# Graph stack on one core: the end of layers 0 and 1 in another order, piece loads issued by ScalarE, stores and indices by SyncE, first loads of the recurrence in parts

## The chip, the cores and the metric

The kernel runs on one core of one Trainium2 chip. A core has TensorE (PE in the profile), VectorE (DVE), ScalarE (ACT), GpSimd (POOL) and SyncE (SP), and 16 DMA engines to which SP, ACT and POOL can give transfers. The metric is the device time of one execution in microseconds (us); lower is better.

## The reference

Sixteen graphs (B = 16) of 1024 nodes (N) with 256 features (D) pass through four layers, in float32. Each layer adds its output to x. All weights and the dense adjacency matrix `adj` (about 3% of its entries are not zero) are inputs.

```
for each layer: h = relu(layernorm(x)); x = x + layer(h)
layer 0: u = adj * exp(e_i + f_j + a_b); a = u / row sum of u; out = a @ (h W_w^T + W_b)
layer 1: d = (row sum of adj + 1e-5)^-0.5; out = d_i adj d_j @ (h weight) + bias
layer 2: for i in 0 .. N-1, one after the other:
             p = (adj^T scaled by 1/deg)[i] @ h        # uses the rows of h already replaced
             r, z = sigmoid(split(x_i W_ioux^T + b + p W_iouh^T + b'))
             hc = tanh(x_i W_coux^T + b + (p * r) W_couh^T + b')
             h[i] = z * p + (1 - z) * hc
layer 3: out = silu(rmsnorm(((eps h + adj @ h) W1 + b1))) W2 + b2
```

## The kernel before, in words

`layers_0_1` computes layers 0 and 1 and prepares layer 2; in the profiled execution it fills about 1463 of 4587 us. `layer_2` is the recurrence, then layer 3 follows. The text calls an iteration of `layers_0_1` a stage.

**Stages.** The loop over i has a stage for each graph. `sums` multiplies the adjacency of graph i with a 1024 x 256 operand in seven products of quarters (a Strassen-like scheme: the quarters `b11`, `b21`, `b22`, `t1` to `t4` are tiles `at`, products go to the PSUM banks `px`, `py`, `pz`, sums to `ag`). It is called twice a stage: with the operand of layer 0 (tile `q`) and with that of layer 1 (tile `h1`). The operand's differences s1 and s2 are made by VectorE in `combos` (L358, L359); product "s2" is the third, and begins with a matmul named px<-at,s. In `sums` (L374 is the matmul) ScalarE copies px into `ag` (L380, L387, L393) and VectorE adds or subtracts the other banks (L384, L394, L398, L401).

**Hooks.** `sums` takes seven functions, one called after each product: a0, a1, a2_, a3 to a6 in the first call, d0 to d6 in the second. They hold everything else a stage does: loads of the next graph (`load_x`, `get`), statistics (`Moments`), additions of quarters by an accumulating DMA of POOL (`plus`, L294), and `plus_row` (L349), which adds a row vector to a quarter of x on POOL: `W_b` for layer 0, `bias` for layer 1, four pairs each.

**After each call.** `weights` (L410, L413) multiplies `ag` by the layer's weights and adds to x: layer 0 of graph i after the first call, layer 1 of graph i - 1 there too (`second_weights`), in pairs of node tiles. `normed` (L345, ScalarE) gives h1, and, after the second call, h2 of graph i - 1, the input of layer 2. `inv_sqrt` (L83, POOL) makes the scales `rs`. x after layer 1 is stored to `x2_d` (L707), h2 to `he_d` (L789).

**An order for the recurrence.** The generator `orders` runs beside the stages on VectorE: `side(us)` in a hook takes its next steps up to a cost. `places` puts the 128 nodes of each node tile into bins (o_fit L129 to L134); `rest` (L155 and on) makes indices, stores them to `order_d` (L176), reads them back as `table` (L181), then makes a second assignment (L197, L198) and picks (o_top, o_open, o_most, o_need). Both read a part of the adjacency, `own`, in pieces of four rows of `pc` (256 KB): `fetch` (L101) issues one, two ahead of its use in `piece` (L106); three buffers hold them. Of 64 pieces, 32 are for `places`, 32 for `rest`.

**Jobs.** From stage 9 on a `Job` for each graph prepares layer 2's data, two a stage (run_a and run_b): `load` (L490, L492, L495), `mask` and `scale` (on POOL, L503 to L511), `turn` (permutes h2 by transposes, L521 to L526, and stores `heT_d`, L527), `first` (L533), `order` (L545 to L556: permutes adjacency tiles, stores `near_d` and `next_d`), `base` (L562 to L565, stores `base_d`). Jobs 14 and 15 come in a last iteration i = 16, after the second sums of graph 15: the tail. All of these stores are issued by POOL.

**The recurrence's start.** `layer_2` issues on SP the loads of its weights (`wx`, L821), biases, `he` (L950, from heT_d), `bxt` (L1156, from base_d) and `wh`; `hs<-he` (L991) on POOL feeds its first matmuls (L1000).

Each engine runs its instructions in the order in which the program writes them (`manual_schedule`); waits between engines and for tile buffers follow from the data.

Of the kernel before, what the change touches and what calls it, by code (L numbers as in the profile page):

```python
# [16 lines left out]
P = 128  # L17
# [23 lines left out]
def gnn_stack(ctx: ExitStack, tc: tile.TileContext, a: dict, out: bass.AP):  # L41
# [51 lines left out]
    def orders(pool, psum):  # L93
# [5 lines left out]
        def fetch(j0):  # L99
            nz = pool.tile([P, R, P], F32, name="pc", bufs=3)  # L100
            nc.gpsimd.dma_start(nz, a["own"][:, j0 : j0 + R])  # L101
            pieces.append(nz)
# [14 lines left out]
        def places():  # L117
# [4 lines left out]
            fetch(0)  # L122
            fetch(R)
            yield 9.0
            for j0 in range(0, P, R):
# [12 lines left out]
                if j0 + 2 * R < P:  # L138
                    fetch(j0 + 2 * R)
# [15 lines left out]
        def rest():  # L155
# [14 lines left out]
            for k in range(2):  # L170
# [8 lines left out]
                with nc.allow_non_contiguous_dma(reason="indices, once"):  # L179
                    for g in range(G2):  # L180
                        nc.gpsimd.dma_start(table[k][:, g].rearrange("p t s -> p (t s)"),  # L181
                                            order_d[k].rearrange("t s b i -> (b i) (t s)")[g * GR : (g + 1) * GR])
# [7 lines left out]
            fetch(0)  # L190
            fetch(R)
            yield 9.0
            for j0 in range(0, P, R):
# [8 lines left out]
                if j0 + 2 * R < P:  # L202
                    fetch(j0 + 2 * R)
# [48 lines left out]
        yield from places()  # L252
        yield from rest()
# [5 lines left out]
    def layers_0_1():  # L259
        with ExitStack() as st:  # L260
# [13 lines left out]

            load_x(0, 2)
            we = big.tile([P, DC, D + 1], F32, name="ad")
# [200 lines left out]
            class Job:  # L477
# [51 lines left out]
                def first(self):  # L529
# [6 lines left out]
                    del h2[b]  # L536
# [30 lines left out]
                def rest(self):  # L567
                    self.first()
                    self.order()
                    self.base()  # L570

            math = orders(big, psum)
            left = [0.0]

            def side(us):
                left[0] += us * 1.25
                while left[0] > 0:
                    cost = next(math, None)
                    if cost is None:
                        break  # L580
                    left[0] -= cost
                left[0] = min(left[0], 0.0)
# [36 lines left out]
            jobs[16] = (Job(14, {"ao": "at5"}), Job(15, {"ad": "at0", "ab": "at1", "to": "at2", "hT": "at3", "ao": "at4"}))  # L619

            for i in range(B + 1):
# [4 lines left out]
                def a0():  # L626
# [4 lines left out]
                    if i:  # L631
                        plus_row(x[i], "W_b", 1)
                    side(1.0)
                def a1():
                    if ahead:
                        get(i + 1, "b11", 0, 0)
                    if i:
                        plus_row(x[i], "W_b", 2)
                    second()
                    add_halves(i, "t4", "t2", "b21")  # L640
                def a2_():
                    if ahead:
                        get(i + 1, "t1", 0, 1)
                    if i:
                        plus_row(x[i], "W_b", 3)
                    side(3.4)
                def a3():
                    side(2.6)
                def a4():
                    if ahead:  # L650
# [27 lines left out]
                else:  # L678
                    run_a.load()
                    run_b.load()  # L680
                    run_a.mask()
                    run_a.scale()
                last = i == B
                mv2 = small.tile([P, NT, 2], F32, name="mv")

                def second_weights(pairs):
                    if behind:
                        weights(x[i - 1], ags[i - 1], w1, dis[i - 1],
                                (lambda t: stats(x[i - 1], (t,), mv2)) if last else (lambda t: None), pairs)
                pairs = list(range(0, NT, 2))  # L690
                if run_a:
                    run_a.turn()
                else:
                    second_weights(pairs[:2])
                    pairs = pairs[2:]
                if here:
# [6 lines left out]
                    if ahead:  # L703
                        mean[i + 1].root()
                second_weights(pairs)
                if behind:
                    nc.gpsimd.dma_start(rows(x2_d[i - 1]), x[i - 1])  # L707
                if last:
                    rs2 = inv_sqrt(small, mv2[:, :, 1], LN_EPS, [P, NT], "rs")
                    run_a.rest()  # L710
                    shift = small.tile([P, NT], F32, name="shift")
# [953 lines left out]
```

## Time and profile before

| what | value |
|---|---|
| median of three runs | 4593.31 us (4590.48, 4593.31, 4597.71) |
| profiled execution, its own time | 4588.57 us |
| its span in the trace | 4586.7 us |
| granted TensorE clock, mean | 0.974 |
| stages 1 to 8 start at | 99.6, 178.0, 256.1, 334.8, 412.8, 491.6, 562.9, 641.0 us |
| stages 9 to 15 start at | 712.3, 802.4, 908.5, 1017.2, 1126.2, 1226.0, 1325.2 us |
| second sums of graph 15 end | 1398.5 us |
| first load of the recurrence (wx, L821) issued | 1463.65 us |

The page's first section gives each engine's busy time, its share of the span, and the number of instructions. In the lists of waits each line names the engine and line that waited, what ended the wait, the total in us, the number of times and the longest. In a timeline a line is: start in us, duration in us, engine, source line, operation, output<-input, count. A line such as L374 is one of the kernel's file. The profile comes from one execution, so sums made from it stand against that execution's own time.

### The profile page before, as it was taken

The numbers are of one execution on the slowest core, as the hardware profiler recorded it, in microseconds if no ns is written. First come the engines' busy times: TensorE is split into PE (matmuls) and PEld (weight loads), VectorE is DVE, ScalarE is ACT, GpSimd is POOL, SyncE is SP. The second block draws the span as 40 slices with busy tenths as digits, with TensorE's granted clock in tenths as the row PEclk, the third lists the DMA queues.
The fourth block names the chain that finished last, engine by engine and source line by source line (L and its number), as shares of the span: only waits on it lengthen the run. The fifth ranks groups of instructions, "written<-read, shape, count | busy, mean of one in ns | idle before, by whom it ended". The sixth has DMA issues, their size and how long they took to land. (4 is left out here: it accounts for less than half of the span.)

```text
span 4586.7 us, 55389 instructions
## 1 busy us (share of the span) xinstructions
PE 4255.1 (93%) x18967; PEld 2921.0 (64%) x18967; DVE 2718.0 (59%) x6213; ACT 1606.4 (35%) x3861; POOL 1653.1 (36%) x1880
## 2 busy tenths in 40 slices
PE   7999999888896999999999999999799999999998
PEld 3544455444554777777777878787556656565656
DVE  7888877577752444444444444446366666666765
ACT  2454545333432232322232323233233343333333
POOL 2232323543434323232323323324243444444352
PEclk9999999999997999999999999999899999999999
DMA  5354446766546544444344444541232222222310
GB/s 190 119 155 152 148 137 204 211 221 220 202 159 212 163 141 151 145 148 153 126 142 152 127 156 146 166 135 63 74 130 91 103 83 101 92 92 85 109 47 19
DMA packets 355108, 627.15 MB, mean 137 GB/s; under 512 B 42016, under 2 KB 259744, under 8 KB 336288
## 3 DMA queue, kind: packets, MB, share of 16 engines
q1 hardware_dynamic: 314208, 462.36, 30.2%
q0 software_dynamic: 40480, 159.68, 11.4%
q8 instruction: 204, 3.34, 0.3%
q14 instruction: 216, 1.77, 0.1%
HBM read 488.52 MB, written 116.65 MB: 132 GB/s over the span
## 5 line engine op out<-in xcount | busy, mean ns | idle before, releaser
L888 PE MATMUL pf<-hb,ab 128*128 128x256 f32 x1568 | 407.9, 383 | 16.5 <-DMA hb<-hs_d 7.2
L1000 PE MATMUL pf<-hs,wx 128*128 128x256 f32 x1536 | 349.8, 382 | 22.4 <-POOL hs L991 20.8
L1000 PEld LDWEIGHTS pf<-hs,wx 128*128 128x128 f32 x1536 | 291.3, 192 | 65.9 <-POOL hs L991 22.6
L888 PEld LDWEIGHTS pf<-hb,ab 128*128 128x128 f32 x1568 | 280.5, 191 | 68.6 <-issue 14.0
L1454 PE MATMUL ph<-bxt,hb 128*128 128x512 f32 x704 | 312.4, 600 | 6.4 <-ACT hb L1438 5.6
L1483 POOL TENSOR_TENSOR ss<-ss,sq 128x512 f32<-128x512 f32 x224 | 280.5, 1271 | 88.6 <-ACT sq L1481 84.9
L83 POOL TENSOR_TENSOR rs<-rs_v,mhalf 128x8 f32<-128x8 f32 (+1 forms) x65 | 112.4, 1729 | 551.8 <-DVE rs_v L79 368.8
L410 PE MATMUL pmm<-w,ag 128*128 128x256 f32 x1024 | 242.2, 393 | 33.7 <-DVE x L413 17.4
L1288 POOL DMA_INDIRECT hs_d<-h,table x128 | 128.9, 1007 | 339.6 <-ACTq L1274 162.5
L410 PEld LDWEIGHTS pmm<-w,ag 128*128 128x128 f32 x1024 | 196.9, 196 | 80.8 <-DVE x L413 29.8
L1544 PEld LDWEIGHTS po<-w,hh 128*128 128x128 f32 x2048 | 236.0, 193 | 9.5 <-issue 7.2
L1544 PE MATMUL po<-w,hh 128*128 128x128 f32 x2048 | 240.2, 277 | 1.4 <-ACT hh L1527 0.7
L1454 PEld LDWEIGHTS ph<-bxt,hb 128*128 128x128 f32 x704 | 133.8, 193 | 168.2 <-issue 160.8
L1005 DVE TENSOR_TENSOR gates<-pf,bias 128x512 f32<-128x512 f32 x128 | 88.2, 690 | 237.8 <-PE pf L1000 237.8
L1526 DVE TENSOR_TENSOR hh<-hh,po 128x512 f32<-128x512 f32 x256 | 154.4, 678 | 96.7 <-PE po L1523 96.7
L1095 ACT ACTIVATE r<-pr 128x256 f32<-128x256 f32 (+3 forms) x230 | 68.0, 347 | 403.1 <-PE pr L1054 387.7
L1481 ACT ACTIVATE sq<-hh 128x512 f32<-128x512 f32 x224 | 141.2, 630 | 164.3 <-DVE hh L1479 125.3
L1036 PE MATMUL pf<-bd,h 128*128 128x384 f32 (+4 forms) x512 | 185.8, 455 | 4.6 <-ACT bs L875 2.8
L1039 DVE TENSOR_TENSOR bxt<-bxt,pf 128x384 f32<-128x384 f32 (+4 forms) x256 | 124.8, 500 | 97.6 <-PE pf L1036 96.1
L1479 DVE SCALAR_TENSOR_TENSOR hh<-ph,b,u 128x512 f32<-128x512 f32 x192 | 144.0, 751 | 64.8 <-PE ph L1475 54.5
L1112 DVE TENSOR_TENSOR w<-w,hc 128x256 f32<-128x256 f32 (+3 forms) x230 | 87.4, 380 | 138.8 <-ACT hc L1111 138.7
L337 ACT ACTIVATE pt<-x,m_neg 128x256 f32<-128x256 f32 x240 | 114.3, 476 | 151.1 <-DVE m_neg L332 144.8
(351 smaller groups left out, 9528.5 us busy)
## 6 DMA issues: line engine op xcount, KB each, us to landing
at<-in_quarters SPq DMA_DIRECT2D x80, 1024.0 KB, 11.5
ab<-in_columns SPq DMA_DIRECT2D x127, 512.0 KB, 3.8
bxt<-in_adjT SPq DMA_DIRECT2D x88, 512.0 KB, 5.9
at<-at POOLq DMA_DIRECT2D x30, 1024.0 KB, 8.9
at<-in_adjT SPq DMA_DIRECT2D x40, 512.0 KB, 6.8
pc<-in_own POOLq DMA_DIRECT2D x64, 256.0 KB, 6.7
x_d<-x POOLq DMA_DIRECT2D x16, 1024.0 KB, 4.9
he_d<-h POOLq DMA_DIRECT2D x16, 1024.0 KB, 12.8
```

Of the source, the lines that this page charges most:

```text
L410: nc.tensor.matmul(po[:, t - t0], ag[:, c, t * P : (t + 1) * P], w[:, c], start=c == 0, stop=c == DC - 1)
L888: nc.tensor.matmul(pb, ab[:, jts[k]], hb[:, jts[k]], start=k == 0, stop=k == len(jts) - 1)
L1000: nc.tensor.matmul(pg[:, e], wx[:, c, q * D + e * P : q * D + (e + 1) * P], self.hs[:, c], start=c == 0, stop=c == DC - 1)
L1036: nc.tensor.matmul(pf, h[:, g, c * P : (c + 1) * P], bd[:, g, b0 : b0 + n, S : S + far], start=True, stop=True)
L1039: return lambda: nc.vector.tensor_add(to, to, pf)
L1288: nc.gpsimd.indirect_dma_start(out=hs_d[t][g][:, :], out_offset=row(1, g, t, s), in_=h[:, g], in_offset=None)
L1454: nc.tensor.matmul(pa, h[b][:, mt, c * P : (c + 1) * P], at[b][n0 // NH][:, mt], start=mt == 0, stop=mt == NT - 1)
L1479: nc.vector.scalar_tensor_tensor(hh[q][:, k], ph, b1[:, k : k + 1], u, op0=ALU.add, op1=ALU.add)
L1481: nc.scalar.activation(sq, hh[q][:, k], AF.Square)
L1483: nc.gpsimd.tensor_tensor(ss[q], ss[q], sq, ALU.add)
L1526: nc.vector.tensor_mul(hh[q][:, k], hh[q][:, k], pr)
L1544: nc.tensor.matmul(po[:, n], left[:, c, n * P : (n + 1) * P], right[:, c], start=onto is None and n == 0 and c == 0, stop=c == HH - 1, ski ...
```

## The change

1. `fetch` hands its load to a list, `later`, which the next `side` empties; ScalarE issues it (`nc.scalar.dma_start`). Three pieces are fetched ahead in place of two; the buffers stay three.
2. The stores to `x2_d` and `he_d` and the loads of `table` are issued by SP in place of POOL. Each of the four loads of `table` is followed by a step boundary of cost 5.0.
3. `plus_row` moves: W_b pairs 1 to 3 from a0, a1, a2_ to a2_, a3, a4; bias pairs 0 to 3 from d0 to d3 to d2, d3, d4, d6.
4. In stages 9 to 15 `run_a.turn` stands after `normed` of h1, between the two halves of `second_weights`, in place of ahead of them.
5. Iteration i = 16 is gone. After the second sums of graph 15 an order written out by hand runs jobs 13, 14 and 15 in turns, with buffers named for them.
6. In `layer_2` the loads of `he` for t = 0 and of `bxt` are split by graph: 0 to 13, 14, 15.
7. The setup tile `we` takes a buffer of the name "x".

The core of the diff:

```diff
@@ -97,9 +97,11 @@
         def fetch(j0):
-            nz = pool.tile([P, R, P], F32, name="pc", bufs=3)
-            nc.gpsimd.dma_start(nz, a["own"][:, j0 : j0 + R])
-            pieces.append(nz)
+            def run():
+                nz = pool.tile([P, R, P], F32, name="pc", bufs=3)
+                nc.scalar.dma_start(nz, a["own"][:, j0 : j0 + R])
+                pieces.append(nz)
+            later.append(run)
@@ -119,8 +121,8 @@
             nc.vector.memset(held, 0.0)
-            fetch(0)
-            fetch(R)
+            for j0 in range(0, 3 * R, R):
+                fetch(j0)
             yield 9.0
@@ -135,8 +137,8 @@
                         yield 1.0
-                if j0 + 2 * R < P:
-                    fetch(j0 + 2 * R)
+                if j0 + 3 * R < P:
+                    fetch(j0 + 3 * R)
                 yield 1.2
@@ -176,10 +178,11 @@
                 yield 9.0
-                with nc.allow_non_contiguous_dma(reason="indices, once"):
-                    for g in range(G2):
-                        nc.gpsimd.dma_start(table[k][:, g].rearrange("p t s -> p (t s)"),
-                                            order_d[k].rearrange("t s b i -> (b i) (t s)")[g * GR : (g + 1) * GR])
+                for g in range(G2):
+                    with nc.allow_non_contiguous_dma(reason="indices, once"):
+                        nc.sync.dma_start(table[k][:, g].rearrange("p t s -> p (t s)"),
+                                          order_d[k].rearrange("t s b i -> (b i) (t s)")[g * GR : (g + 1) * GR])
+                    yield 5.0
@@ -249,8 +252,12 @@
-        yield from places()
-        yield from rest()
+        later = deque()
+
+        def work():
+            yield from places()
+            yield from rest()
+        return work(), later
@@ -272,8 +279,8 @@
+            we = big.tile([P, DC, D + 1], F32, name="x", bufs=3)
             load_x(0, 2)
-            we = big.tile([P, DC, D + 1], F32, name="ad")
             nc.sync.dma_start(we[:, :, :D], a["W_w"].rearrange("(c p) d -> p c d", p=P))
@@ -533,7 +540,6 @@
                     nc.scalar.activation(self.bs, pb[:, :D], AF.Copy, scale=dinv[:, b, 0:1])
-                    del h2[b]
@@ -568,11 +574,14 @@
                     self.base()
-
-            math = orders(big, psum)
+                    del h2[self.b]
+
+            math, later = orders(big, psum)
             left = [0.0]
...
             def side(us):
+                while later:
+                    later.popleft()()
                 left[0] += us * 1.25
@@ -616,9 +625,11 @@
             jobs = {i: (Job(2 * (i - 9)), Job(2 * (i - 9) + 1)) for i in range(9, 16)}
-            jobs[16] = (Job(14, {"ao": "at5"}), Job(15, {"ad": "at0", "ab": "at1", "to": "at2", "hT": "at3", "ao": "at4"}))
-
-            for i in range(B + 1):
+            jobs[15][1].names = {"ao": "h1"}
+            job14 = Job(14, {"ad": "at6", "ab": "ds", "to": "at0", "hT": "q", "ao": "hT"})
+            job15 = Job(15, {"hT": "h1", "ao": "q"})
+
+            for i in range(B):
                 run_a, run_b = jobs.get(i, (None, None))
@@ -628,25 +639,25 @@
                         run_a.load()
-                    if i:
-                        plus_row(x[i], "W_b", 1)
                     side(1.0)
...
                         get(i + 1, "b11", 0, 0)
-                    if i:
-                        plus_row(x[i], "W_b", 2)
                     second()
...
                     if i:
-                        plus_row(x[i], "W_b", 3)
+                        plus_row(x[i], "W_b", 1)
                     side(3.4)
                 def a3():
+                    if i:
+                        plus_row(x[i], "W_b", 2)
                     side(2.6)
                 def a4():
+                    if i:
+                        plus_row(x[i], "W_b", 3)
                     if ahead:
@@ -675,24 +686,13 @@
                     rs = inv_sqrt(small, mv[:, :, 1], LN_EPS, [P, NT], "rs")
-                else:
-                    run_a.load()
-                    run_b.load()
-                    run_a.mask()
-                    run_a.scale()
-                last = i == B
-                mv2 = small.tile([P, NT, 2], F32, name="mv")
...
                     if behind:
-                        weights(x[i - 1], ags[i - 1], w1, dis[i - 1],
-                                (lambda t: stats(x[i - 1], (t,), mv2)) if last else (lambda t: None), pairs)
+                        weights(x[i - 1], ags[i - 1], w1, dis[i - 1], pairs=pairs)
                 pairs = list(range(0, NT, 2))
-                if run_a:
-                    run_a.turn()
-                else:
-                    second_weights(pairs[:2])
-                    pairs = pairs[2:]
+                second_weights(pairs[:2])
+                pairs = pairs[2:]
                 if here:
@@ -702,22 +702,11 @@
                         mean[i + 1].root()
+                if run_a:
+                    run_a.turn()
                 second_weights(pairs)
                 if behind:
-                    nc.gpsimd.dma_start(rows(x2_d[i - 1]), x[i - 1])
-                if last:
-                    rs2 = inv_sqrt(small, mv2[:, :, 1], LN_EPS, [P, NT], "rs")
-                    run_a.rest()
-                    shift = small.tile([P, NT], F32, name="shift")
-                    nc.vector.scalar_tensor_tensor(shift, mv2[:, :, 0], -1.0, rs2, op0=ALU.mult, op1=ALU.mult)
-                    h2[i - 1] = big.tile([P, NT, D], F32, name="h2", bufs=2)
-                    normed(h2[i - 1], x[i - 1], shift, rs2, all_)
-                    nc.gpsimd.dma_start(rows(he_d[i - 1]), h2[i - 1])
-                    run_b.mask()
-                    run_b.scale()
-                    run_b.turn()
-                    run_b.rest()
-                    break
+                    nc.sync.dma_start(rows(x2_d[i - 1]), x[i - 1])
                 if run_a:
@@ -732,19 +721,17 @@
                         get(i + 1, "t3", 0, 1)
-                    plus_row(x[i], "bias", 0)
                     if m2:
...
                 def d1():
-                    plus_row(x[i], "bias", 1)
                     second1()
...
                 def d2():
-                    plus_row(x[i], "bias", 2)
+                    plus_row(x[i], "bias", 0)
                     if m2:
@@ -752,12 +739,13 @@
                 def d3():
-                    plus_row(x[i], "bias", 3)
+                    plus_row(x[i], "bias", 1)
                     if ahead:
...
                 def d4():
+                    plus_row(x[i], "bias", 2)
                     if ahead:
@@ -772,10 +760,13 @@
                 def d6():
+                    plus_row(x[i], "bias", 3)
                     if m2:
...
                 ags[i] = sums(i, left_of, [d0, d1, d2, d3, d4, d5, d6], lambda name: drop(i, name))
+                if not ahead:
+                    break
                 if run_b:
@@ -786,7 +777,7 @@
                     normed(h2[i - 1], x[i - 1], m2.shift, m2.rs, all_)
-                    nc.gpsimd.dma_start(rows(he_d[i - 1]), h2[i - 1])
+                    nc.sync.dma_start(rows(he_d[i - 1]), h2[i - 1])
                     if i - 1 < 14:
@@ -795,8 +786,39 @@
                 side(5.0 if run_a else 3.0)
+            h2[14] = big.tile([P, NT, D], F32, name="h2", bufs=2)
+            normed(h2[14], x[14], m2.shift, m2.rs, all_)
+            nc.sync.dma_start(rows(he_d[14]), h2[14])
+            job14.load()
+            mv = small.tile([P, NT, 2], F32, name="mv")
+            weights(x[15], ags[15], w1, dis[15], lambda t: stats(x[15], (t,), mv))
+            nc.sync.dma_start(rows(x2_d[15]), x[15])
+            rs = inv_sqrt(small, mv[:, :, 1], LN_EPS, [P, NT], "rs")
+            run_b.first()
+            run_b.turn()
+            shift = small.tile([P, NT], F32, name="shift")
+            nc.vector.scalar_tensor_tensor(shift, mv[:, :, 0], -1.0, rs, op0=ALU.mult, op1=ALU.mult)
+            job14.mask()
+            run_b.order()
+            run_b.base()
+            job14.scale()
+            h2[15] = big.tile([P, NT, D], F32, name="h2", bufs=2)
+            normed(h2[15], x[15], shift, rs, all_)
+            nc.sync.dma_start(rows(he_d[15]), h2[15])
+            job15.load()
+            job14.first()
+            job14.turn()
+            job14.base()
+            job15.mask()
+            job15.turn()
+            job15.first()
+            job15.base()
+            job15.scale()
+            job14.order()
+            job15.order()
             for _ in math:
-                pass
+                while later:
+                    later.popleft()()
@@ -944,10 +966,13 @@
+            parts = ((0, B - 2), (B - 2, B - 1), (B - 1, B))
+
             def load_he(t):
                 he = big.tile([P, DC, B, P], F32, name="he")
-                for c in range(DC):
-                    nc.sync.dma_start(he[:, c], heT_d[:, :, c, t * P : (t + 1) * P].rearrange("b p i -> p b i"))
+                for b0, b1 in parts if t == 0 else ((0, B),):
+                    for c in range(DC):
+                        nc.sync.dma_start(he[:, c, b0:b1], heT_d[b0:b1, :, c, t * P : (t + 1) * P].rearrange("b p i -> p b i"))
                 return he
@@ -1152,8 +1177,9 @@
                 bxt = shared.tile([P, DC, B, P], F32, name="bxt")
-                for c in range(DC):
-                    nc.sync.dma_start(bxt[:, c], base_d[:, :, c].rearrange("b p i -> p b i"))
+                for b0, b1 in parts:
+                    for c in range(DC):
+                        nc.sync.dma_start(bxt[:, c, b0:b1], base_d[b0:b1, :, c].rearrange("b p i -> p b i"))
                 load_w(wh, "W_iouhT", "W_couhT")
...
                     task()()
...
```

The hunks at `chain` in `rest` change its fetches as those of `places`.

More of the change, by code (lines that the diff above doesn't have):

```diff
@@ L189, in rest @@
             nc.vector.memset(chain, 1.0)
-            fetch(0)
-            fetch(R)
+            for j0 in range(0, 3 * R, R):
+                fetch(j0)
             yield 9.0
@@ L201, in rest @@
                         yield 1.2
-                if j0 + 2 * R < P:
-                    fetch(j0 + 2 * R)
+                if j0 + 3 * R < P:
+                    fetch(j0 + 3 * R)
                 yield 1.6
```

## The prediction

> **What bounds the kernel now.** First the page's busy times.
>
> ```profile
> PE 4255.1 (93%) x18967; PEld 2921.0 (64%) x18967; DVE 2718.0 (59%) x6213; ACT 1606.4 (35%) x3861; POOL 1653.1 (36%) x1880
> ```
>
> TensorE is busy for 93% of the span, so an edit pays only where it takes away a gap of TensorE. The diff adds and removes no matmul. I therefore listed what TensorE waited for in each stretch of layers 0 and 1: stages 1 to 8 (100 to 770 us), then stages 10 to 15 (802 to 1400 us). Columns: total us, times, longest.
>
> ```profile
> PE pz L374 <- DVE ag L394: 15.6, 7, 4.6
> PE px L374 <- DVE o_fit L129: 13.0, 5, 3.5
> PE px L374 <- DVE s L359: 7.0, 3, 2.3
> ```
>
> ```profile
> PE px L374 <- issue: 15.1, 3, 6.1
> PE pmm L410 <- DVE x L413: 14.2, 3, 12.0
> PE pt L521 <- DVE hT L526: 12.8, 5, 5.3
> PE pmm L410 <- DVE ag L401: 6.8, 2, 4.4
> PE pmm L410 <- DVE ag L398: 6.8, 2, 5.0
> ```
>
> "o_fit" and "issue" only name what DVE did last; I looked for what held DVE. The timeline around the second sums of stage 4 (start us, us, what):
>
> ```profile
> 383.27 0.95 POOL L707 DMA_DIRECT2D x_d<-x  x1
> 384.83 1.63 POOL L349 TENSOR_TENSOR x<-x,bias_sb 128x512 f32<-128x512 f32 x1
> 386.04 0.93 POOL L101 DMA_DIRECT2D pc<-in_own  x1
> 386.64 4.05 POOL L349 TENSOR_TENSOR x<-x,bias_sb 128x512 f32<-128x512 f32 x3
> 387.06 4.20 DVE L359 TENSOR_TENSOR s<-s,h 128x512 f32<-128x512 f32 x1
> ```
>
> L359 takes 692 ns elsewhere in this stage. Here it takes 4.20 us and ends with POOL's third addition, and TensorE starts px<-at,s 2.2 us late. In stages 10 to 13 DVE itself waits, for POOL and for pieces (waits of DVE, then of POOL):
>
> ```profile
> DVE rd L698 <- POOL rs L83: 17.0, 6, 14.1
> DVE pc L106 <- DMA pc<-in_own: 16.9, 4, 6.5
> ```
>
> ```profile
> POOL table L181 <- issue: 22.9, 3, 8.5
> ```
>
> Last the tail: stretches of the windows view (length, busy PE, PEld, DVE, ACT, POOL, clock, DMA share, GB/s), SP's waits before the recurrence's first load (L821) and TensorE's longest wait there:
>
> ```profile
> 1325.20:1398.50 73.30, 71.89 (x244) 41.68 (x243) 34.75 (x71) 19.04 (x51) 29.43 (x26) 1.00 0.41 144
> 1398.50:1463.60 65.10, 38.56 (x180) 29.84 (x178) 21.64 (x45) 16.18 (x31) 25.83 (x30) 0.78 0.52 197
> 1463.60:1493.00 29.40, 15.25 (x47) 10.94 (x48) 4.34 (x10) 2.88 (x6) 10.94 (x15) 0.67 1.05 296
> ```
>
> ```profile
> SPq L821 <- DMA near_d<-at: 5.8, 1, 5.8
> SPq L821 <- DMA next_d<-at: 1.4, 1, 1.4
> ```
>
> ```profile
> PE pf L1000 <- POOL hs L991: 20.8, 3, 16.7
> ```
>
> Stage 15 is dense; the 65 us after it are 59% busy at a lower clock. Then everything waits for POOL's last stores to land.
>
> **What the Trainium skill says.** "SBUF — State Buffer", section "Who interferes with whom": a VectorE instruction with two SBUF inputs and a GpSimd instruction that reads SBUF lock each other out for a whole instruction. The trace agrees (692 ns against 4.20 us), and shows more: DVE got in only after three POOL additions in a row. "DMA: Bandwidth & Descriptors", section "Issuing engines are not separate DMA queues": another issuing engine saves its sequencer's time alone. Its section "Queues, rings and completion order" adds that a DMA engine takes its queues in turn, packet by packet, so a piece on ScalarE's queue need not stand behind POOL's stores. The trace has pieces landing in 2.8, 7.3 and 13.5 us (least, median, most, stages 10 to 14), the one issued at 912.1 us behind near, next and base after 12.2 us; no transfer on ScalarE's queue is in this trace. "TensorE: Matmul & The Clock Gate", section "What's actually happening": the clock halves after an idle window of some 3.4 us. The 0.78 above agrees, so a gap removed in stages 10 to 13 gives back a little more than itself.
>
> **The change part by part**, against the profiled execution (4588.6 us; the median of the three times, 4593.3, is 4.7 above it).
>
> *A. Bias additions, stages 1 to 8.* x_d's store (0.95 us) and the pieces (0.93) leave POOL; the order of instructions puts three additions directly after POOL's accumulate DMA and the fourth after a later rs. In stage 4: 383.3 + 0.95 + 1.63 + 2 x 1.35 = 388.5, then s takes 0.7: 389.2, which is when py ends. The eight gaps at px<-at,s are 3.52, 2.19, 2.19, 2.19, 2.88, 2.33, 2.35, 2.34 = 20.0 us; I keep 0.6 in each: **-15** (-19 to -8). Next late is ag's copy from ACT.
>
> *B. W_b additions.* They move from hooks a0 to a2 to a2 to a4. POOL runs in order and its inputs are long there, so all four run back to back: one lock of about 5.5 us in place of 2 + 4.5. The gaps at pz<-at,q in stages 1 to 5 are 1.17, 2.60, 4.65, 3.30, 3.30 = 15.0; DVE gains 1 us a stage: **-3** (-10 to +2: the lock comes at another moment).
>
> *C. Table loads, stage 10.* Four of 2.75 us and 22.9 us of waits between them leave POOL; rs no longer stands behind them, and the 12.0 us gap of pmm goes: **-12** (-15 to -5). On SP they stand ahead of the x loads of stages 10 and 11. Their issue there isn't in the trace: between 0.4 us (an x load) and 8 us (POOL's wait for one), paid by loads that SP issues a stage ahead of use, so 0 (to +5).
>
> *D. Pieces, stages 11 to 13.* Three ahead in place of two, off POOL's ring. DVE's 16.9 us for pieces show in TensorE as "issue" 6.15 + 5.48 + 3.48 = 15.1, and in part again as ag L398 and L401 and hT L526 (26.4 together), since DVE stays late. The 15.1 go if a fetch lands within three pieces, which 13.5 us allows; of the rest I take 2. **-17** (-35 to -4: DVE does the same work and is busy 81 of stage 12's 109 us by the windows view).
>
> *E. The turn placed between weight pairs; chain parts moved 0.7 of a stage later.* The same instructions; the wait for hT L526 has more cover, but o_top's and o_open's transposes come together before stage 15. **-1** (-3 to +3). he_d's and x2_d's stores go to SP, whose next x load waits for the same h already: 0.
>
> *F. The tail.* I laid the new order on the durations of before. TensorE ends stage 15's weights 7 us after its second sums, first/turn/order/base of job 13 at 20.5, first/turn/base of 14 at 29, turn/first/base of 15 at 40, the orders of 14 and 15 at 48. POOL's last next store is then issued at 50 and lands 4.6 later, at 54.4: the gate falls from 65.2 us (1463.65) to about 55: **-10** (-16 to -4). Of the old waits 9.19 (hT behind next_d's landing) and 3.67 (hT behind heT_d's) go; new is scale of 15 on POOL (3.6 us) ahead of the last order.
>
> *G. First loads in parts.* 2 + 2 loads become 6 + 6. The parts are to start before graphs 14 and 15 are done, but wx (L821) stands ahead of them on SP and still waits for everything in layers 0 and 1. So they gain nothing, and 8 more issues of about 0.45 us, partly under the 8 to 10 us landings, cost **+1** (0 to +3).
>
> *H. Fetches on ACT.* 64 issues at SP's 0.33 to 0.46 us lie in an engine 35% busy. But each waits for DVE's last use of its buffer, and ACT's copies of px into ag stand behind that; L394 and then TensorE wait for them. The trace bounds neither side: **+3** (0 to +60).
>
> Sum: -15 -3 -12 -17 -1 -10 +1 +3 = -54; 4588.6 - 54 + 4.7 = **4539 us**. The low ends of A to F give -98 (4495).
>
> **Rivals.**
> 1. *Slower: fetches block ACT.* If a fetch waits t on the path, the change costs 64t against 57 us of gains: 0.9 us each cancels them, from 1.03 us the kernel is slower by over 0.2% (the 9 us that a measurement here can tell from none), and 1.3 us gives 4593 + 83 - 57 = 4619. For it: ACT had no DMA before, and DVE runs up to a lock late. Against: fetches are given out after a piece is used, so the buffer has been free for a moment, and ACT's copies wait for px themselves (up to 4.0 us at L380). Chance 0.13: 0.09 beyond 1.03 us, 0.04 near 0.9.
> 2. *DVE stays the bound.* DVE's stage work is unchanged (69.4 of 78.4 us in stage 1, windows view), locks only move: A gives 5, B 0, D 4, with C and F: -5 -12 -4 -10 +4 = -27, 4566 us. Chance 0.25.
> 3. *The end doesn't do what it says*: F as G, the last next landing as late as now; 4549 us, inside my range. Chance 0.15.
> 4. *More*: stages 10 to 14 lose most of their 79 us of idle, C and D at their ends: about 4510 us. Chance 0.14.
>
> My forecast as it stands has 0.33. The range takes in the forecast, rivals 2 and 3 and the nearer half of 4, which leaves 0.20 out: 4498 to 4582. Faster by over 0.2% 0.87, within 0.2% 0.04, slower 0.09.
>
> **What would show it.** A: L359 near 0.7 to 1.5 us and no px<-at,s gap of 2 us in stages 1 to 8. C: no 12 us gap of pmm in stage 10. D: stages 11 to 13 each about 6 to 10 us shorter than 108.7, 108.9 and 99.9, DVE's wait for pieces gone. F: L821 at some 55 us after the last second sums. G: the he and bxt parts issued after L821, in one row. H and rival 1: waits of ACT's queue for DVE pc with ACT's copies late behind them, DVE L394 waiting longer for ACT. I am wrong if stages 1 to 8 keep their lengths of 71 to 79 us, or if any stage grows.

## The result, and the profile after

The changed kernel took 4561.37 us (median of five, 4557.53 to 4565.99) against 4593.31 before; the ratio is 0.9934, 95% interval 0.9919 to 0.9948. A second timing on another occasion gave 0.9932 (0.9918 to 0.9945), with a median of 4555.75. The profiled execution took 4557.89 us with a span of 4556.2, so 30.5 us of span went, where 54 were forecast. First the busy times of the page, after the change:

```profile
PE 4244.7 (93%) x18967; PEld 2920.8 (64%) x18967; DVE 2697.2 (59%) x6213; ACT 1607.6 (35%) x3861; POOL 1585.5 (35%) x1780
```

TensorE issues the same 18967 matmuls and is busy 10 us less; the section on the prediction comes back to that. The waits of TensorE in stages 1 to 8, after (engine, line, what ended the wait: total us, times, longest):

```profile
PE pmm L417 <- DVE x L420: 7.8, 5, 2.0
PE pt L153 <- DVE o_pos L150: 3.0, 1, 3.0
PE pz L381 <- DVE ag L401: 2.7, 6, 0.7
```

The two groups that led this list, pz and px<-at,s, are down to 2.7 us and nothing; the wait of pmm for x has grown from 3.2 to 7.8. In stages 10 to 15 the list has a new head:

```profile
PE pt L528 <- DVE hT L533: 24.9, 11, 3.0
PE pt L528 <- ACT hT L531: 20.4, 11, 3.3
PE pmm L417 <- DVE ag L405: 7.9, 3, 4.1
PE pt L234 <- DVE o_most L235: 7.9, 1, 7.9
```

The 12 us gap of pmm and the 15 us under "issue" are gone as forecast (1.2 us is left of the latter), but the transposes of the turn (pt L528; L521 before) now wait 45 us, where they waited 20 (12.8 and 7.5). And o_most, the end of VectorE's chain, is waited for at the end of stage 14.

The tail, in the stretches that answer to those of before: stage 15, then to wx's issue, then 29.4 us more.

```profile
1290.90:1372.30 81.40, 75.79 (x243) 43.75 (x243) 38.33 (x111) 18.86 (x51) 21.33 (x18) 0.93 0.24 82
1372.30:1427.20 54.90, 35.98 (x180) 28.73 (x178) 21.31 (x45) 16.31 (x31) 24.12 (x27) 0.82 0.66 234
1427.20:1456.60 29.40, 15.01 (x52) 11.42 (x53) 4.99 (x11) 2.88 (x6) 11.00 (x15) 0.69 1.06 298
```

The middle stretch is 54.9 us long against 65.1; the last one does the same work in the same time.

To see where in a stage the time lies I cut each stage, in every trace, at the first matmul px<-at and at the end of the last matmul of each call of `sums`: first sums, middle (weights, turn, jobs), second sums, end. Sums over stages, in us (a cut can be 0.2 us off):

| | before | changed | turn_back | no_yields | best1 | half_yields | turn_last | turn_alone |
|---|---|---|---|---|---|---|---|---|
| stages 1 to 8, all | 612.7 | 570.0 | 569.7 | 569.7 | 570.0 | 569.8 | 569.8 | 611.1 |
| first sums, 9 to 15 | 212.8 | 187.5 | 186.1 | 204.5 | 206.9 | 189.2 | 186.9 | 214.8 |
| middles, 9 to 15 | 202.3 | 237.0 | 189.3 | 237.6 | 182.8 | 187.4 | 211.9 | 250.0 |
| second sums, 9 to 15 | 174.0 | 171.1 | 171.0 | 169.9 | 169.9 | 171.4 | 173.8 | 176.0 |
| ends, 9 to 14 | 97.3 | 105.1 | 108.5 | 92.0 | 92.0 | 91.9 | 105.2 | 96.7 |

Up to the recurrence's first matmul into `pr` the change gains 36.9 us (1485.0 to 1448.1): +2 in the startup, -42.7 in stages 1 to 8 (-24.6 in first sums, -25.2 in second sums, +7.0 in middles, where TensorE waits for x), +14.3 in stages 9 to 15 (that is -25.3 in first sums, +34.7 in middles, -2.9 in second sums, +7.8 in ends), -10 from there to wx's issue. The other 6.4 us came back in the recurrence, which the change does not touch after its first loads: from its 200th matmul into `pr` to its last it took 1391 us before and 1398 in this profile, and between 1388 and 1395 in the profiles of the experiments.

### The profile page after: what moved, and what is told of

It is laid out like the page before. It is cut to its first block, busy times and chain, and to the rows that moved or that the text cites. A ratio compares the mean times of both kernels' runs of the same rounds, so it can differ in the third digit from the quotient of the medians.

```text
span 4556.2 us, 55386 instructions
## 1 busy us (share of the span) xinstructions
PE 4244.7 (93%) x18967; PEld 2920.8 (64%) x18967; DVE 2697.2 (59%) x6213; ACT 1607.6 (35%) x3861; POOL 1585.5 (35%) x1780
## 5 line engine op out<-in xcount | busy, mean ns | idle before, releaser
L417 PE MATMUL pmm<-w,ag 128*128 128x256 f32 x1024 | 253.2, 403 | 28.6 <-DVE x L420 14.0
L1552 DVE TENSOR_TENSOR hh<-hh,po 128x512 f32<-128x512 f32 x256 | 154.5, 685 | 96.7 <-PE po L1549 96.7
L1553 ACT ACTIVATE hh<-hh,rw 128x512 f32<-128x512 f32 x256 | 160.4, 712 | 15.2 <-DVE hh L1552 15.2
```

What stands on the lines that cost most here:

```text
L417: nc.tensor.matmul(po[:, t - t0], ag[:, c, t * P : (t + 1) * P], w[:, c], start=c == 0, stop=c == DC - 1)
L1552: nc.vector.tensor_mul(hh[q][:, k], hh[q][:, k], pr)
L1553: nc.scalar.activation(hh[q][:, k], hh[q][:, k], AF.Silu, scale=rw[:, k : k + 1])
```

## The experiments

Two theories stood against each other after the result. **Theory 1**: the turn behind `normed` costs what the rest gains, because its copies stand behind `normed` on ScalarE and behind the wait for rs on VectorE. **Rival**: VectorE's chain was pushed into later stages, and the turn only shows that. The timeline of stage 12 in the changed kernel:

```profile
1012.49 1.04 PE L528 MATMUL pt<-to,h 128*128 128x128 f32 x8
1013.68 1.64 POOL L83 TENSOR_TENSOR rs<-rs_v,mhalf 128x8 f32<-128x8 f32 x1 [14.15 <-DVE rs_v L79]
1015.71 0.68 DVE L533 COPY hT<-pt 128x512 f32<-128x512 f32 x1
1015.81 4.05 ACT L352 ACTIVATE h<-x,shift,rd 128x256 f32<-128x256 f32 x8 [8.48 <-DVE rs_v L81]
1016.45 0.66 PE L528 MATMUL pt<-to,h 128*128 128x128 f32 x4 [2.92 <-DVE hT L533]
1019.76 1.05 ACT L531 COPY hT<-pt 128x512 f32<-128x512 f32 x2
1020.38 1.12 PE L528 MATMUL pt<-to,h 128*128 128x128 f32 x4 [3.28 <-ACT hT L531]
```

Two buffers of pt are filled by 1013.5. VectorE may empty the second only after rd and shift, which wait for POOL's rs; ScalarE may empty the first only after `normed`'s eight activations. TensorE stands still for 2.92 and then 3.28 us, with two ready weight pairs behind it in its order.

**turn_back** puts the turn back, in the changed kernel, and with it the two pairs of second weights that had gone ahead of `normed`.

```diff
-                second_weights(pairs[:2])
-                pairs = pairs[2:]
+                if run_a:
+                    run_a.turn()
+                else:
+                    second_weights(pairs[:2])
+                    pairs = pairs[2:]
...
-                if run_a:
-                    run_a.turn()
                 second_weights(pairs)
```

> The changed kernel with one part undone: run_a.turn again ahead of normed and of all second weights in stages 9 to 15. Theory 1 (the turn's copies into hT queue behind normed's eight activations on ScalarE and behind VectorE's wait for rs, so TensorE stalls before pt<-to,h in each of seven stages): those waits fall from 45 us back to about 20, the stretch from the end of the first sums to the start of the second shrinks from 30 to 38 us to 25 to 31 us, and the kernel is 20 to 40 us faster than the change (4561): 4521 to 4541. Rival 2 (those stretches are longer because VectorE's chain of pieces was moved later into stages 11 to 14, and the turn only shows it): within 8 us of 4561. Rival 3 (the old place brings back another wait of the same size, TensorE for rs and x): 4555 to 4570 with waits for DVE x in place of hT.

Measured: 4506.27 us, ratio 0.9812 (0.9795 to 0.9828), 50 to 55 us faster than the change. The same place in its trace:

```profile
985.67 1.04 PE L528 MATMUL pt<-to,h 128*128 128x128 f32 x8
986.35 0.59 ACT L531 COPY hT<-pt 128x512 f32<-128x512 f32 x1 [1.62 <-issue]
986.99 0.66 PE L528 MATMUL pt<-to,h 128*128 128x128 f32 x4 [0.28 <-ACT hT L531]
```

ScalarE is free and copies at once. From stage 10 on the waits for hT fall from 45.3 to 17.7 us; the middles of stages 9 to 15 fall from 237.0 to 189.3. Of these 47.7 us, 34.3 are idle time of TensorE, and 32.6 of that stood at the turn (pt L528), so the order of the weight pairs has little part in it; 13.4 are busy time of the same matmuls (the mean clock of stages 9 to 14 is 0.95 with the turn moved, 0.97 without). Theory 1 holds, and the cost is larger than its own estimate.

**turn_alone** makes this one part of the change in the kernel before.

```diff
-                if run_a:
+                if last:
                     run_a.turn()
                 else:
                     second_weights(pairs[:2])
                     pairs = pairs[2:]
...
                         mean[i + 1].root()
+                if run_a and not last:
+                    run_a.turn()
                 second_weights(pairs)
```

> The kernel before with one part of the change alone: run_a.turn behind normed, between the two halves of the second weights, in stages 9 to 15 (4587 without it on this chip, by the runs so far). Theory 1 (the place of the turn costs what putting it back gave in the changed kernel, 50 to 55 us): 4630 to 4645, the stretch between first and second sums 5 to 9 us longer in each of the seven stages. Rival (in the kernel before VectorE is late in these stages anyway, so its lateness covers part of it): 4597 to 4625.

Measured: 4637.5 us, ratio 1.0103 (1.0086 to 1.0120), 48 us slower than before. Its middles are 47.7 us longer, and the same two waits lead TensorE's list from stage 10 on:

```profile
PE pt L521 <- DVE hT L526: 41.1, 11, 15.8
PE pt L521 <- ACT hT L524: 20.1, 11, 3.3
```

The part costs about the same with and without the rest of the change; the rival is out.

**turn_last** leaves the turn behind `normed` and puts it behind all second weights.

```diff
-                if run_a:
-                    run_a.turn()
                 second_weights(pairs)
+                if run_a:
+                    run_a.turn()
```

> The changed kernel with run_a.turn behind all second weights in place of between their halves (it stays behind normed in ScalarE's order). Theory 1 (the stall is TensorE standing at the turn while ScalarE still does normed's 4 us and VectorE waits for rs; 7 us of weights in front of it cover that): 30 to 50 us faster than the change, 4508 to 4530. Rival (any place behind normed delays the turn's copies and with them first, order and the next loads): 4535 to 4560.

Measured: 4531.13 us, ratio 0.9876 (0.9859 to 0.9892): 25 to 30 us faster than the change, 1 us outside theory 1's numbers, and 25 us slower than turn_back. The weights cover part of the stall; the waits for hT at the turn are still 24.3 us from stage 10 on. The rival has a part too: TensorE now waits 9.0 us for ScalarE's copies of `order` (pt L551 and L568), which in turn_back it does not.

**no_yields** takes the four step boundaries out, so that the chain ends earlier.

```diff
                                           order_d[k].rearrange("t s b i -> (b i) (t s)")[g * GR : (g + 1) * GR])
-                    yield 5.0
```

> The changed kernel without the four step boundaries of cost 5.0 behind the table loads. Theory 1 (these boundaries push the chain of pieces 0.7 of a stage later, and its end, o_most, then stands at the end of stage 14 with a 7.9 us gap of TensorE and 12 us more there than before): the end of stage 14 is 8 to 12 us shorter, stage 10 is 3 to 8 us longer since VectorE does the work there: 0 to 8 us faster than 4561. Rival (the place of the chain makes no difference, VectorE's sum of work is the same): within 3 us of 4561, with the gap moved to stage 10 or 13. Rival (stage 10 needs the boundaries, since the table loads on SP are late or VectorE is the bound there): 5 to 15 us slower.

Measured: 4551.28 us, ratio 0.9908 (0.9888 to 0.9928), which overlaps the interval of the change. By the table the ends give back 13.1 us and the first sums take 17.0. From the start of stage 1 to the end of stage 15's second sums it is 1273.7 us against 1270.7 and 1272.9 in two profiles of the change, so the lower median isn't from there. **best1** does the same together with turn_back.

> The changed kernel with run_a.turn in its old place and without the four step boundaries of cost 5.0. Theory 1 (the turn's stalls and the late end of the chain are separate costs): 4506 less the 0 to 10 us of the boundaries, 4496 to 4506, with the end of stage 14 at 14 to 16 us (28 with the boundaries). Rival (with the turn's stalls gone the stages are 48 us shorter in all, so VectorE has less room and the chain that starts earlier lengthens the first sums of stages 11, 12 and 14 by as much as the end of stage 14 gives back): 4504 to 4520.

Measured: 4504.07 us, ratio 0.9819 (0.9805 to 0.9832), the same as turn_back: the rival's answer. The gap at the end of stage 14 goes and first sums of 31, 35 and 37 us come. **half_yields** tries a place between, with the turn back.

```diff
-                    yield 5.0
+                    yield 2.5
```

> The changed kernel with run_a.turn in its old place and the four boundaries at 2.5 in place of 5.0. With 5.0 it took 4506, without them 4504; with 5.0 the chain's end stands at the end of stage 14 (28 us there against 14), without them the first sums of stages 11, 12 and 14 take 31, 35 and 37 us against 26. Theory 1 (VectorE's chain costs about the same wherever it lies): 4500 to 4510. Rival (a place between the two avoids both costs): 4488 to 4499.

Measured: 4493.71 us (4486.82 to 4505.13), ratio 0.9796 (0.9773 to 0.9820). By the table it has the short first sums of the one and the short ends of the other, 566.5 us for stages 9 to 14 against 580.9 (turn_back) and 578.2 (best1). It is the lowest median and beats both kernels; its interval overlaps those of turn_back and best1, so the step from them to it is read from the traces.

The next three take stages 1 to 8 apart. **plus_back** puts `plus_row` into its old hooks.

```diff
                         run_a.load()
+                    if i:
+                        plus_row(x[i], "W_b", 1)
                     side(1.0)
...
                         get(i + 1, "b11", 0, 0)
+                    if i:
+                        plus_row(x[i], "W_b", 2)
                     second()
...
                         get(i + 1, "t3", 0, 1)
+                    plus_row(x[i], "bias", 0)
                     if m2:
...
                 def d1():
+                    plus_row(x[i], "bias", 1)
                     second1()
...
```

> The changed kernel with plus_row in the hooks of before (W_b 1 to 3 in a0, a1, a2_; bias 0 to 3 in d0 to d3). Theory 1 (the lock between POOL's additions and VectorE's two-input instructions set the gaps at px<-at,s and pz<-at,q, and it is the move that takes it off them): stages 1 to 8 take back most of their 43 us, so 20 to 40 us slower than 4561. Rival (it is the removal of the piece loads and of x_d's store from POOL's queue that lets the additions run early; the hooks hardly matter, since POOL runs them back to back anyway): 0 to 10 us slower.

Measured: 4570.86 us, ratio 0.9952 (0.9935 to 0.9968). Stages 1 to 8 take 579.3 us, 9.3 more than in the change, all of it in the second sums (209.0 against 199.0): in these stages it is the rival's size.

**pieces_pool** issues the pieces from POOL, three ahead.

```diff
-                nc.scalar.dma_start(nz, a["own"][:, j0 : j0 + R])
+                nc.gpsimd.dma_start(nz, a["own"][:, j0 : j0 + R])
```

> The changed kernel with the piece loads issued by POOL again, still three ahead and through the list. Theory 1 (in stages 11 to 13 a piece on POOL's queue stands behind near, next, base and the accumulate, and in stages 1 to 5 its issue splits POOL's additions): 8 to 25 us slower than 4561, VectorE's wait for pieces back at 5 to 17 us. Rival (three ahead is what removes the wait, the queue is not important): within 5 us of 4561. Rival (ScalarE's issues with their waits ahead of the px copies cost more than they give): 3 to 15 us faster.

Measured: 4580.77 us, ratio 0.9984 (0.9973 to 0.9994), 19 to 25 us slower than the change: 13.1 in stages 1 to 8 and 12.6 in 9 to 14. The first sums of stages 11 to 13 take 90.5 us, against 81.4 in the change and 99.2 before. VectorE's wait for pieces from stage 10 on, in the change and then here:

```profile
DVE pc L108 <- DMA pc<-in_own: 2.0, 2, 1.3
```

```profile
DVE pc L108 <- DMA pc<-in_own: 15.8, 3, 7.8
```

From stage 10 on, then, three ahead on POOL's queue does not remove the wait. In stages 1 to 8 it does: VectorE waited 12.0 us for pieces there before, and not at all here. Two ahead on ScalarE's queue was not tried.

**stores_pool** gives the stores of x2_d and he_d in the loop back to POOL.

```diff
-                    nc.sync.dma_start(rows(x2_d[i - 1]), x[i - 1])
+                    nc.gpsimd.dma_start(rows(x2_d[i - 1]), x[i - 1])
...
-                    nc.sync.dma_start(rows(he_d[i - 1]), h2[i - 1])
+                    nc.gpsimd.dma_start(rows(he_d[i - 1]), h2[i - 1])
```

> The changed kernel with the stores to x2_d and he_d issued by POOL again in the loop (the table loads stay on SP). Theory 1 (x2_d's store of 0.95 us stands ahead of the bias additions, so their lock ends 1 us later and the gap at px<-at,s comes back in part): 0.5 to 1 us in each of stages 1 to 8 and 4 to 12 us slower in all, against about 4561. Rival (SP's stores delay its loads by more than POOL's time is worth): 3 to 10 us faster. Rival (neither is on the path): within 3 us.

Measured: 4567.68 us, ratio 0.9962 (0.9949 to 0.9976). Stages 1 to 8 take 584.1 us, 14.1 more than in the change, of it 11.5 in second sums and 2.4 in first sums; the whole is 6 to 12 us slower than the change, theory 1's size. In stage 4 x2_d's store takes 0.95 us of POOL ahead of the bias additions, which begin 1.9 us after POOL's last rs against 0.6 in the change, and TensorE waits 1.39 us at px<-at,s.

**tail_old** puts the old tail into the changed kernel (the iteration i = 16 as before, stores on SP).

```diff
-            for i in range(B):
+            for i in range(B + 1):
...
-                if not ahead:
-                    break
...
-            h2[14] = big.tile([P, NT, D], F32, name="h2", bufs=2)
...
-            job15.order()
```

> The changed kernel with the tail of before: after the second sums of graph 15 again an iteration i = 16 with its turn, weights and rest, job 14 then job 15; its stores of x2_d and he_d stay on SP. Theory 1 (the new order itself takes 10 us off the time from the last second sums to wx's issue, as the two profiles show, 65.0 and 54.9 us): 7 to 13 us slower than the change (4556 to 4561), that is 4563 to 4574, with 62 to 68 us in that place. Rival (the stores on SP and POOL's shorter queue give the 10 us, the order doesn't matter): within 3 us of the change.

Measured: 4565.29 us, ratio 0.9950 (0.9934 to 0.9967). From the last second sums to wx's issue it takes 65.4 us (1371.6 to 1437.0), against 54.9 and 55.6 in two profiles of the change. The order gives the 10 us; this is read from the traces, since the interval overlaps that of the change.

**parts_off** loads he and bxt whole.

```diff
-            parts = ((0, B - 2), (B - 2, B - 1), (B - 1, B))
+            parts = ((0, B),)
```

> The changed kernel with the loads of he (t = 0) and bxt whole again. Theory 1 (the parts gain nothing, since wx ahead of them on SP still waits for the last landing of graph 15): within 3 us of the change, and from wx's issue to the first matmul pr<-x about 21 us, as in both kernels (21.4 before, 20.9 after). Rival (the parts let hs<-he start on part of the data and gain): 4 to 10 us slower without them. Rival (more issues cost): 3 to 5 us faster without them.

Measured: 4556.35 us, ratio 0.9938 (0.9925 to 0.9952); from wx's issue to the first matmul into `pr` 20.4 us. The parts neither gain nor cost anything that shows. **after_again** is the changed kernel a second time.

> The changed kernel itself, to be read beside the others on the same chip. By its first timing it is 0.9934 of before. The recurrence from its 200th matmul pr<-x to the last took 1391 us in the profile of before and 1398 in that of the change, though no instruction of it differs: if that is spread from run to run, this profile shows 1388 to 1396; if the change causes it, 1397 or more.

Measured: 4555.75 us, ratio 0.9932 (0.9918 to 0.9945); the recurrence took 1391 us from its 200th matmul into `pr` to its last. The 7 us that it was longer in the first profile are spread from run to run.

## Why the prediction was right or wrong

The measured time lies in the range, and the direction is right. But two steps were wrong by far, in opposite directions (25 us too small, 47 too optimistic), so that it lies in the range is in part luck. One of its own signs of being wrong came true: it named "if any stage grows", and stages 9, 13 and 14 grew (90.1 to 97.4, 99.8 to 102.9, 99.2 to 113.0 us); stage 12, which was to lose 6 to 10 us, lost 0.6. Step by step, predicted and measured:

| step | predicted | measured | from |
|---|---|---|---|
| A, second sums of stages 1 to 8 | -15 | -25.2 | the two traces |
| B, first sums of stages 1 to 8 | -3 | -24.6 | the two traces |
| middles of stages 1 to 8 | no term | +7.0 | the two traces |
| C, table loads | -12 | -15 | middle of stage 10: 38.4 before, 23.2 in turn_back; not undone alone |
| D, pieces | -17 | -18 | first sums of stages 11 to 13: 99.2 and 81.4; see below |
| E, the turn | -1 together | +48 | turn_back, turn_alone |
| E, the chain's place | | -2 | stage 14: first sums -9.5; ends of 9 to 14 +7.8 |
| F, tail | -10 | -10 | the two traces, tail_old |
| G, parts | +1 | 0 | parts_off |
| H, fetches on ACT | +3 | not seen | pieces_pool |

**E failed as a step.** It costed the moved turn by its instructions, which are the same, and said that its wait had "more cover". It didn't ask what the turn was moved behind on each engine that serves it. ScalarE's copies came behind 4 us of activations that themselves wait for VectorE and POOL, and the turn stands in TensorE's order in front of work that was ready. That was to be read from before: the timeline shows `normed` as a block of eight activations, and pt has two buffers for four groups of transposes. Of turn_back's 38.4 us in stages 9 to 14 (619.3 to 580.9), TensorE's busy time gives 8.3 (531.5 to 523.2, the same 1953 matmuls) and idle time the rest.

**A and B were too small for two reasons.** The first is the clock. Slices of 3.5 us of the kernel before, around the 4.65 us gap in stage 3 (length, busy PE, PEld, DVE, ACT, POOL, clock, DMA share, GB/s):

```profile
282.50:286.00 3.50, 2.60 (x3) 1.17 (x4) 3.22 (x18) 0.00 (x0) 2.21 (x2) 0.50 0.00 0
286.00:289.50 3.50, 3.50 (x7) 1.52 (x6) 3.15 (x17) 0.00 (x0) 0.00 (x1) 0.67 0.30 75
289.50:293.00 3.50, 3.50 (x18) 3.09 (x17) 3.24 (x15) 2.54 (x9) 0.00 (x0) 1.00 0.00 0
```

The gap is followed by matmuls at half clock. In stages 1 to 8 TensorE's busy time falls from 569.5 to 553.9 us for the same 1797 matmuls, so 15.6 of the 42.7 us are busy time and 27 are gaps; the mean clock of these stages rises from 0.97 to 1.00. The prediction quoted the Trainium skill on this ("TensorE: Matmul & The Clock Gate", "What's actually happening": the clock halves after an idle window of some 3.4 us), used it for stages 10 to 13, said "a little more", and put no term for it into A and B. Here shorter gaps did it too: 2.19 us at px<-at,s in stage 2 was followed by 3.5 us at a clock of 0.53.

The second is a wait that no term holds. B took the gaps at pz<-at,q for the lock's, and D counted waits for pieces in stages 10 to 13 alone. But VectorE waited for pieces in stages 2 to 5 as well; in the kernel before, stages 1 to 8, then stage 4:

```profile
DVE pc L106 <- DMA pc<-in_own: 12.0, 4, 4.0
```

```profile
355.56 0.23 DVE L106 TENSOR_SCALAR pc<-pc 128x144 f32<-128x144 f32 x1 [2.98 <-DMA pc<-in_own]
360.05 0.68 DVE L394 TENSOR_TENSOR ag<-pz,ag 128x512 f32<-128x512 f32 x1
360.79 6.67 PE L374 MATMUL pz<-at,q 128*128 128x512 f32 x8 [3.30 <-DVE ag L394]
```

The rows of the late piece stand ahead of L394 in VectorE's order, and TensorE waits for L394. The waits are 1.10, 3.88, 2.98 and 4.03 us in stages 2 to 5, and some 5 us after each follows a gap at pz<-at,q of 2.60, 4.65, 3.30 and 3.30. First sums of these four stages give 22.2 of the 24.6 us. With three pieces ahead no such wait is left there, with ScalarE issuing (the change) or POOL (pieces_pool, first sums 216.5). This fits every trace, but two ahead in the changed kernel was not tried.

It was not the hooks (with `plus_row` in its old hooks first sums stay at 214.0), and it was not he_d's store on its own, though that (a move that E set at 0) is what cuts the lock in two. Before, the store waited 3.18 us for h in POOL's queue in stage 4, and three of the four additions ran behind it (341.34 to 345.06). In the change the four run as one block at the start of the stage, and VectorE is locked out for all of them:

```profile
319.38 5.63 DVE L131 SCALAR_TENSOR_TENSOR o_fit<-o_below,o_bins,o_open 128x16 f32<-128x16 f32 x1
319.73 5.23 POOL L356 TENSOR_TENSOR x<-x,W_b_sb 128x512 f32<-128x512 f32 x4
```

The one lock is about as long as B said (5.6 us against 5.5). In stores_pool it is cut again, in stage 4:

```profile
330.29 0.97 POOL L780 DMA_DIRECT2D he_d<-h  x1 [3.20 <-ACT h L352]
330.77 4.25 DVE L133 SCALAR_TENSOR_TENSOR o_held<-o_open,o_bins,o_held 128x16 f32<-128x16 f32 x1
331.27 3.71 POOL L356 TENSOR_TENSOR x<-x,W_b_sb 128x512 f32<-128x512 f32 x3
```

Yet its first sums are 216.3. A's mechanism held: L359 (L366 after) takes 0.69 us in all of stages 1 to 8; the lock now falls on the instruction ahead of it (L365, 2.84 us in stage 4), earlier than TensorE needs the result. The 20.0 us of gaps at px<-at,s are gone, where A kept 0.6 in each; the clock gives the rest. Putting back hooks, pieces or stores costs 10.0 to 11.5 us in second sums each.

**C, D and F came out at their sizes.** F did so by its own working: TensorE's work and POOL's last stores came when it said, the gate 54.9 us after the second sums. One wait in it is new: TensorE stands 4.7 us at job 14's `turn`, behind ScalarE's copy of job 14's `first` into `bo`, which waits 5.6 us for base_d's store of job 13 out of the same buffer. D is right in part by luck. With the pieces back on POOL's queue 9.1 of its 17.8 us come back (90.5), as late pieces would have it; but without the four step boundaries, ScalarE still issuing, the first sums of stages 11 to 13 are 89.9 (no_yields), so that some of the gain is the place of the chain. The section of "DMA: Bandwidth & Descriptors" that was quoted says that another issuing engine saves its sequencer's time alone. On POOL that time is not small: an issue takes 0.56 us, and from stage 10 on POOL stood 38.5 us in pieces_pool until VectorE gave a buffer free, ahead of its other work; the issuing queue was worth 19 to 25 us. Whether pieces also land sooner from ScalarE's queue is open, since the trace has no landings for them.

**The rivals.** Rival 1 (fetches block ScalarE) is out: with the pieces on POOL the kernel is slower. ScalarE's copies do stand behind fetches for up to 8.9 us at a time, but the gap at pz<-at,q that would show it is 2.3 us in all from stage 10 on. Rival 2's time (4566) was near, its reason was not: the locks did come off the path. Rival 3 is out, the tail gives its 10 us (tail_old). Rival 4's time (4510) is that of turn_back, 4506: it is what the change gives without the moved turn, though half of that gain lies in stages 1 to 8 and not in stages 10 to 14.

## What to carry to other kernels

When a step moves within a fixed order, list what then stands in front of it on every engine that serves it, and what ready work then stands behind it: seven turns of unchanged instructions cost 48 us. A DMA on a compute engine's queue holds the compute behind it, and what that costs depends on what follows: by the trace of stores_pool he_d's store, which waited 3.2 us in stage 4, cost 2.4 us in the first sums of eight stages, and x2_d's, 0.95 us of issue ahead of the bias additions, 11.5 in the second. A gap of TensorE can have a second price in the clock: with 27 us of gaps went 15.6 us of slower matmuls. And when a gap is put down to one cause, look through the waits of the engine that ended it for another: here the lock stood in view, and the late pieces behind it were missed.

## What the runs showed of the hardware

- Between 1.9 and 3.0 us the length of a gap of TensorE does not decide what the clock does after it. In the first 3.5 us or so after gaps of 1.94 us (stage 2, changed), 2.19 and 2.95 us (stages 2 and 7, before) it was 0.57, 0.53 and 0.52; after gaps of 2.33 and 2.34 us (stages 6 and 8, before) and 2.96 us (stage 7, changed) it was 1.00.
- Four additions of POOL in a row kept one VectorE instruction of 0.23 us waiting for all four (5.63 us).
- Pieces of 256 KB issued by ScalarE took 0.33 us of its queue, by POOL 0.56 us.
